# Column copies on VectorE written as one-element maxima, with loads, sums and column counts rearranged, in a one-core graph-network kernel

## The chip, the core and the metric

The kernel runs on one core of one Trainium2 chip. The metric is the device time of the whole program in microseconds. Before the change it is 4877.81 us, the median of three runs (4875.6 to 4879.19). The profile comes from one further execution, taken with the hardware profiler on; that execution took 3555.16 us. So the profiled execution is shorter than the runs without a profile by 1322.6 us, and both numbers are kept apart in what follows.

The engines are called PE (TensorE), DVE (VectorE), ACT (ScalarE), POOL (GpSimd) and SP (SyncE, which here only issues transfers).

## What is computed

One layer of a graph network over 12500 nodes of 64 features and 400000 edges, sorted by their target node `dst`. For each edge the features of both ends and 16 edge features go through two small layers, the messages are summed by target node, and a third layer, a residual and a layer norm finish it:

```python
m_in = concatenate([x[src], x[dst], edge_attr], axis=-1)      # 400000 x 144
h = silu(m_in @ W1 + b1)
messages = silu(h @ W2 + b2)
agg = segment_sum(messages, dst, num_segments=12500)
out = silu(concatenate([x, agg], axis=-1) @ W3 + b3)
return layernorm(x + out)
```

All of it is in float32.

## The kernel before

**Tiles, octets, windows.** Edges are cut into 3125 tiles of 128. Eight tiles make an octet (391 of them), and 24 tiles, three octets, make a window: since the edges are sorted, all targets of a window lie within 112 neighbouring nodes. A loop in `windows` (L555) goes over the octets as a software pipeline: in step o it issues loads for octet o + 2, gathers for o + 3, the first layer of o, the second layer of o - 1 and the sums of o - 2. The order of instructions on PE, ACT, DVE and SP inside that loop is the order in which the code stands; nothing is rescheduled there.

**First layer.** `x[dst] W1b` is formed once a window for its 112 nodes (`window_product` L353, from a slice `xr` of the transposed x that `window_load` L346 brings), and then spread to the edges by a product with a 0/1 matrix `oh`, which `compare_dst` (L377) makes on DVE; the edge features ride in the same matrix's last 16 rows. `x[src] W1a` is precomputed for all nodes in the first octets (`table`, L171) and stored in DRAM as `pa`. For each tile of an octet one indirect transfer, issued by POOL (`gather`, L332, the instruction at L341), fetches 128 rows of `pa`, one for each edge; PE adds them in by a product with the identity (L415). From octet 9 on (`RAW`) the gathers read `pa`, before that x itself.

**Columns and rows.** Not all rows are gathered. The whole transposed x also lies in SBUF (`xs`, 128 partitions, two copies of the 64 features, loaded piece by piece by `resident`, L167). For some pairs of tiles the kernel copies the column of each edge's source node out of `xs`, four bytes of 64 partitions at a time, at an address that is read from a register, into a tile `cx` (`columns`, L244, the copy at L267); PE then multiplies `cx` with W1a (L412). A pair of tiles takes 256 such columns and saves two gathers. ACT makes 28 + 28 columns an octet and DVE 24 + 24 (`ACOLS`, `VCOLS`), in two bursts each: ACT's ahead of its two activations (L419, L434), DVE's behind its two comparisons (L381, L388). Source addresses are loaded into registers 16 at a time on ACT and up to 128 at a time on DVE (L263). The pairs served so are spaced by `RATE`, the sum of all four numbers. SP serves others by single row transfers (`rows`, L280, 16 an octet).

```python
for e, r in zip(range(e0 % P, e0 % P + n), regs):
    copy(t[h, 4 * e:4 * e + 4], xb[h, ds(r - (XBASE[s] + XADDR), 4)])
```

**Second layer and sums.** PE applies W2 (L430), ACT silu (L434), and `add_up` (L439) sums an octet's messages into the window's 112 nodes by a product with another 0/1 matrix `eh`, made by `compare_nodes` (L385) on DVE from the window's node numbers (`wrow`, kept in PSUM) and the edge's target (`dc`, in SBUF). There are four `eh` buffers. When a window's last octet is summed, DVE adds its sums to `agg` in SBUF (`add_window`, L446). `sums` has two halves, used by even and odd windows.

**Nodes.** When all edges of a group of 512 nodes are done, the third layer, the silu, the statistics and later the division and the store of that group are run between octets; `later` (L522) puts each of them at a fixed octet behind `lead`, the octet at which the needed window begins. There are 25 groups.

**Buffers and queues.** A gather needs a free one of five `ga` tiles, so POOL runs three octets ahead. SP issues, in order, the loads of `dr` (the targets, for `oh`), of `oh`'s edge features, of `xr`, the pieces of `xs`, of the targets `dc` and the row transfers. ACT issues the weights at the start and the 25 stores of `pa`.

At the end of the loop (L612 to L635) DVE checks with a few long instructions that the windows did hold all targets; a general path stands behind that check and isn't taken with this data.

Of the kernel before, what the change touches and what calls it, by code (L numbers as in the profile page):

```python
# [14 lines left out]
OP = mybir.AluOpType  # L15
AX = mybir.AxisListType
PSUM = bass.MemoryType.PSUM
DRAM = bass.MemoryType.DRAM
ENG = mybir.EngineType
# [6 lines left out]
SCT = 240  # L26
AHEAD = 3
RAW = 9
TABLES = 5
ACOLS = (28, 28)  # L30
VCOLS = (24, 24)
ROWS = 16
ALOAD = 16
XBASE = (0, 64 << 18)
XADDR = 35840
# [59 lines left out]
def windows(ctx, tc, ident, badi, pa, x, xt, src_c, src_row, dst_c, dst_row, attr_t, base, w1, b1, w2, b2, w3, b3, out, edges):  # L95
    nc = tc.nc
    N, D = x.shape
# [22 lines left out]
    dc = fast.tile([P, TILES], I32, name="dc")  # L120
# [9 lines left out]
    for s in range(2):  # L130
        h = slice(s * D, (s + 1) * D)
# [12 lines left out]
    for s in range(3):  # L144
        part = const.tile([1, D], BF16, name=f"part{s}")
# [19 lines left out]
    xs = fast.tile([P, NP], F32, name="xs")  # L165

    def resident(s, c):  # L167
        w = min(XC, NP - c)
        nc.sync.dma_start(xs[s * D:(s + 1) * D, c:c + w], xt[:, c:c + w])

    def table(c):  # L171
        n = min(4 * P, N - c)
# [38 lines left out]
    for k in range(3):  # L211
        t = fast.tile([P, D], F32, name=f"xw{k}")
# [3 lines left out]
    octs = []  # L216
# [3 lines left out]

    with tc.tile_pool(name="gat", bufs=AHEAD + 2) as gat, tc.tile_pool(name="drp", bufs=2) as drp, \
            tc.tile_pool(name="hot", bufs=3) as hot, \
            tc.tile_pool(name="ehp", bufs=4) as ehp, \
            tc.tile_pool(name="work", bufs=2) as work, tc.tile_pool(name="win", bufs=2) as win, \
            tc.tile_pool(name="ps1", bufs=2, space=PSUM) as ps1, \
            tc.tile_pool(name="ps2", bufs=2, space=PSUM) as ps2, \
            tc.tile_pool(name="psa", bufs=1, space=PSUM) as psa, \
# [5 lines left out]

        RATE = sum(ACOLS) + sum(VCOLS)
        pairs = []
        while True:
            o = RAW + -(-2 * P * (len(pairs) + 1) // RATE) + 1
# [4 lines left out]
        xb = xs.bitcast(U8)  # L242

        def columns(o, eng, part):  # L244
            if o < RAW:
                return
            lo = (o - RAW) * RATE
            if eng == ENG.Activation:
                lo, n, copy = lo + sum(ACOLS[:part]), ACOLS[part], nc.scalar.copy
            else:  # L250
                lo, n, copy = lo + sum(ACOLS) + sum(VCOLS[:part]), VCOLS[part], nc.vector.tensor_copy
            hi = lo + n
            while lo < hi:
                j, e0 = lo // (2 * P), lo % (2 * P)
                if j >= len(pairs):
                    return
                n = min(hi - lo, P - e0 % P, ALOAD if eng == ENG.Activation else P)
                if pairs[j] not in cols:
                    cols[pairs[j]] = cx.tile([P, P], F32, name="cx")
                t = cols[pairs[j]].bitcast(U8)  # L260
                s = e0 // P
                h = slice(s * D, (s + 1) * D)
                _, regs = nc.values_load_multi_w_load_instructions(  # L263
                    indices[j][0:1, e0:e0 + n], engines=(eng,), min_val=XBASE[s] + XADDR,
                    max_val=XBASE[s] + XADDR + 4 * (N - 1), skip_runtime_bounds_check_because="src names a node")
                for e, r in zip(range(e0 % P, e0 % P + n), regs):
                    copy(t[h, 4 * e:4 * e + 4], xb[h, ds(r - (XBASE[s] + XADDR), 4)])  # L267
                lo += n


# [1 line left out]
        while True:  # L272
            o = RAW + -(-2 * P * (len(rpairs) + 1) // ROWS) + 1
# [31 lines left out]
        def raddress(o):  # L305
            yes, j = rbegun(o)
            if yes:
                nc.vector.tensor_scalar(rindex[j], rindex[j], 4.0 * D, None, op0=OP.mult)
# [37 lines left out]
        def window_load(c):  # L346
            regs = nc.values_load(bi[0:1, c:c + 1], engines=(ENG.SP, ENG.DVE), min_val=0, max_val=N - 1,
                                  skip_runtime_bounds_check_because="dst names a node")
            winreg[c] = regs
            xr = win.tile([D, W], F32, name="xr")  # L350
            nc.sync.dma_start(xr, xt[:, ds(regs, W)])
            winrow[c] = xr

        def window_product(c):
            pw = mis.tile([P, D], F32, name="mm")
            nc.tensor.matmul(pw[0:W, :], winrow[c], w1ab[:, 1, :], start=True, stop=True)  # L356
            winrow[c] = pw
# [19 lines left out]
        def compare_dst(o):  # L377
            c, t0, n, first, last = octs[o]
            n2 = n + n % 2
            dr, oh = loaded.pop(o)  # L380
            nc.vector.tensor_tensor(oh[0:W, :n2 * P], dr[:, :n2 * P], wn[0:W, c:c + 1].to_broadcast([W, n2 * P]),  # L381
                                    op=OP.is_equal)
            hots[o] = [oh]
# [62 lines left out]
        def add_window(c):  # L446
            a = agg[:, ds(winreg[c], W)]
            nc.vector.tensor_tensor(a, a, sums[:, c % 2, :], op=OP.add)  # L448
# [4 lines left out]
        RB = 6  # L453
# [63 lines left out]
        due = [-(-(c + n + LAG) // STEP) for c, n in groups]  # L517
        NO = len(octs)
        lead = {c: o for o, (c, t, n, first, last) in enumerate(octs) if first}
        todo = {}  # L520

        def later(o, f, *a):  # L522
            todo.setdefault(min(o, NO), []).append((f, a))
# [1 line left out]
        early = sum(d < NCH for d in due)  # L525
        rest = early - early % RB
        for q in range(early):
            o = lead[due[q]] + 2
            later(o, node_load, q)
            later(o, node_product, q)  # L530
            later(o, node_silu, q)
            later(o + 1, node_stats, q)
        for q0 in range(0, rest, RB):
            o = lead[due[q0 + RB - 1]] + 2
            later(o + 2, root, q0, q0 + RB)
            later(o + 3, inverse, q0, q0 + RB)
            for r in range(RB):
                later(o + 3 + 2 * r, divide, q0 + r)
                later(o + 4 + 2 * r, store, q0 + r)

        for o in range(min(AHEAD, NO)):
            gather(o)
# [9 lines left out]
        with tc.manual_schedule(engines={ENG.PE, ENG.Activation, ENG.DVE, ENG.SP}):  # L552
            compare_dst(0)
            compare_nodes(0)
            for o in range(NO + 1):  # L555
                if o == 0:
                    sources(0, slice(CT, SCT))
                    nc.sync.dma_start(dc[:, CT:SCT], dst_c[:, CT:SCT])
                for k in parts[2 * o - 2:2 * o] if o else []:
                    n = min(XC, NP - k)  # L560
                    nc.scalar.activation(agg[:, k:k + n], zero.to_broadcast([P, n]), AF.Copy)
                if o < 5:
                    for c in parts[:3] if o == 0 else parts[o + 2:o + 3]:
                        resident(0, c)
                if o == 8:
                    nc.sync.dma_start(dc[:, SCT:], dst_c[:, SCT:])
                if o == RAW:
                    nc.vector.memset(mv, 1.0)
                    nc.vector.memset(eps, 1e-5)
                if 5 <= o < 5 + (len(parts) + 1) // 2:  # L570
                    for c in parts[(o - 5) * 2:(o - 4) * 2]:
                        resident(1, c)
                index(o + 3)
                rload(o + 3)
                if o % (SCT // OT) == 6 and (o // (SCT // OT) + 1) * SCT < TILES:
                    sources(o // (SCT // OT) + 1)
                if o + AHEAD < NO:
                    gather(o + AHEAD)
                if o + 2 < NO:
                    load(o + 2)  # L580
                    if octs[o + 2][3]:
                        window_load(octs[o + 2][0])
                if o + 1 < NO:
                    compare_dst(o + 1)
                columns(o, ENG.DVE, 0)
                if o >= 3 and octs[o - 3][4]:
                    add_window(octs[o - 3][0])
                if o < NO:
                    first_layer(o)
                if o + 1 < NO:  # L590
                    if octs[o + 1][3] and o:
                        window_copy(octs[o + 1][0])
                    compare_nodes(o + 1)
                columns(o, ENG.DVE, 1)
                if o >= 1:
                    for c in tables[(o - 1) * per:o * per]:
                        table(c)
                if o >= 2:
                    add_up(o - 2)
                if o >= 1:  # L600
                    second_layer(o - 1)
                if o + 2 < NO and octs[o + 2][3]:
                    window_product(octs[o + 2][0])
                address(o + 2)
                raddress(o + 2)
                rows(o)
                if o < NO:
                    for f, a in todo.get(o, []):
                        f(*a)
# [25 lines left out]
        nc.vector.tensor_copy(badi, bs)  # L635

        add_up(NO - 1)
        for o in range(NO - 2, NO):
            if octs[o][4]:
                add_window(octs[o][0])  # L640
        for f, a in todo.get(NO, []):
# [262 lines left out]
```

## Time and profile before

| | |
|---|---|
| median of three runs | 4877.81 us |
| profiled execution, its own time | 3555.16 us |
| span of its instructions | 3553.3 us |
| granted PE clock, mean | 0.752 |
| POOL: gathers | 2773, of which 2701 from `pa` and 72 from x |
| ACT: column copies | 21112, busy 2079.2 us |
| DVE: column copies | 18056, busy 1458.6 us |
| DMA engines, mean busy share | about a third, 92 GB/s |

A line of the costliest groups names the source line, the engine, the operation, output and inputs, the count, then the busy time in us and the mean duration of one in ns, and behind the second bar the idle time of the engine just before these instructions with what ended most of it. Durations of copies overlap, so busy time is less than count times duration. In a list of waits each line gives who waited for whom, the total in us, how often, and the longest. A line in order of time begins with the start and the length in us; several instructions of a kind are merged, with their count at the end. A line of one source line's instructions gives the count, the shortest, median and longest duration in ns, and the times of the first and the last start.

The busy shares over the 40 slices of the span are even from the second slice on (PE 7 or 8 tenths, DVE 6 or 7, ACT 7 or 8, POOL 7): the loop over octets is nearly the whole program, and one octet stands for all.

### The profile page before, as it was taken

The page shows a single profiled execution, that of the slowest core. Times are in us where ns is not written, and L with a number is a line of the kernel's source. Part 1 is how long each engine was busy: PE and PEld are TensorE (multiplying, and loading weights), DVE is VectorE, ACT ScalarE, POOL GpSimd, SP SyncE. Part 2 cuts the span into 40 slices and gives each one's busy share as a digit, 9 for nine tenths or more (in the row PEclk, how much of TensorE's full clock was granted, in tenths as well). Part 3 has the DMA queues.
Part 4 walks back from the last instruction along what each step waited for, and adds up shares of the span by engine and source line. Part 5 has one row for each costly group of instructions (what it writes and reads, how often), then busy time and mean ns, then how long its engine had stood idle before and what let it go on. Part 6 is the DMA issues. An engine that isn't in the chain of part 4 may idle for free.

```text
span 3553.3 us, 96997 instructions
## 1 busy us (share of the span) xinstructions
PE 2717.1 (76%) x15387; PEld 1796.0 (51%) x15387; DVE 2551.0 (72%) x19955; ACT 2598.8 (73%) x21941; POOL 2659.2 (75%) x2782
## 2 busy tenths in 40 slices
PE   7877877777777778777777777777877777777786
PEld 5554554555545455455454554544544545545454
DVE  3667767777687677776777777777778777677673
ACT  1568777787787777777877777778778777777772
POOL 7677777777777777777777777777777777777774
PEclk7867777777777777777777777777677777777776
DMA  6433333333333333333333333333333333333331
GB/s 158 131 90 95 86 89 92 84 92 90 88 99 91 91 89 85 95 86 89 96 93 94 91 85 93 91 89 89 86 95 94 90 92 86 91 90 87 90 95 47
DMA packets 199259, 327.19 MB, mean 92 GB/s; under 512 B 94959, under 2 KB 103306, under 8 KB 197722
## 3 DMA queue, kind: packets, MB, share of 16 engines
q1 hardware_dynamic: 96142, 226.51, 20.3%
q0 software_dynamic: 88736, 91.04, 13.8%
q10 hardware_dynamic: 13740, 3.32, 0.4%
q14 instruction: 511, 4.19, 0.4%
q8 instruction: 130, 2.13, 0.3%
HBM read 314.20 MB, written 6.40 MB: 90 GB/s over the span
## 4 chain that ended last, share of the span: by engine, by line
POOL 50%; issue 20%; DMA 17%; PE 12%; ACT 1%; DVE 0%; SPq 0%; ACTq 0%; POOLq 0%; DVEq 0%
POOL ga L341 50%; DMA ga<-pa,sc 16%; PE p L430 3%; PE pg L443 2%; PE p L401 2%; PE p L415 1%; PE mm L177 1%; PE p L428 1%; ACT cx L267 1%; PE mm L477 1%; PE mm L476 1%; DMA ga<-in_x,sc 0%; PE p L410 0%; PE p L412 0%; PE mm L406 0%
## 5 line engine op out<-in xcount | busy, mean ns | idle before, releaser
L341 POOL DMA_INDIRECT ga<-pa,sc x2701 | 2589.9, 959 | 838.8 <-issue 746.9
L267 ACT COPY cx<-xs 64x4 uint8 x21112 | 2079.2, 188 | 216.8 <-issue 172.0
L267 DVE COPY cx<-xs 64x4 uint8 x18056 | 1458.6, 204 | 204.4 <-issue 172.7
L415 PE MATMUL p<-ident,ga 128*128 128x128 f32 x2702 | 616.8, 349 | 784.2 <-DMA ga<-pa,sc 781.4
L415 PEld LDWEIGHTS p<-ident,ga 128*128 128x128 f32 x2702 | 461.4, 233 | 1109.6 <-issue 945.6
L430 PE MATMUL p<-w2d,h 128*128 128x128 f32 x3126 | 621.9, 361 | 0.0
L419 ACT ACTIVATE h<-p,b1s 128x512 f32<-128x512 f32 x391 | 268.2, 686 | 480.6 <-PE p L415 437.4
L430 PEld LDWEIGHTS p<-w2d,h 128*128 128x128 f32 x3126 | 530.0, 256 | 127.0 <-issue 127.0
L401 PE MATMUL p<-oh,xw 128*64 128x512 f32 x1564 | 561.8, 806 | 5.5 <-DMA sc<-in_src_c 5.5
L388 DVE TENSOR_TENSOR eh<-wrow,dc 128x896 f32<-128x896 f32 x391 | 424.7, 1086 | 178.9 <-PE pg L443 165.3
L443 PE MATMUL pg<-eh,m 128*64 128x112 f32 x6250 | 528.5, 329 | 14.0 <-ACT m L434 13.9
L381 DVE TENSOR_TENSOR oh<-dr,wrow 112x1024 f32<-112x1024 int32 x391 | 473.1, 1210 | 28.2 <-DMA dr<-in_dst_row 16.8
L443 PEld LDWEIGHTS pg<-eh,m 128*64 128x64 f32 x6250 | 420.3, 178 | 83.5 <-issue 42.4
L434 ACT ACTIVATE m<-p 128x512 f32<-128x512 f32 x391 | 232.6, 595 | 116.2 <-PE p L430 83.0
L428 PE MATMUL p<-b2r,one 3*128 3x512 bf16 x391 | 190.3, 487 | 0.0
L360 DVE COPY xw<-mm 112x64 f32<-112x64 f32 x131 | 29.0, 222 | 208.5 <-PE mm L356 208.5
L448 DVE TENSOR_TENSOR agg<-agg,pg 128x112 f32 x131 | 35.0, 267 | 193.5 <-PE pg L443 184.8
L412 PEld LDWEIGHTS p<-cx,w1d 128*128 128x128 f32 x306 | 56.7, 233 | 188.6 <-issue 188.6
L401 PEld LDWEIGHTS p<-oh,xw 128*64 128x64 f32 x1564 | 94.0, 165 | 60.3 <-issue 23.7
L483 ACT ACTIVATE z<-mm 128x256 f32<-128x256 f32 (+1 forms) x25 | 9.6, 383 | 115.3 <-PE mm L477 115.3
L412 PE MATMUL p<-cx,w1d 128*128 128x128 f32 x306 | 91.3, 388 | 0.0
L341 POOL DMA_INDIRECT ga<-in_x,sc x72 | 68.1, 946 | 22.7 <-issue 20.6
(73 smaller groups left out, 790.2 us busy)
## 6 DMA issues: line engine op xcount, KB each, us to landing
dr<-in_dst_row SPq DMA_DIRECT2D x390, 448.0 KB
rx<-pa SPq DMA_DIRECT2D x5888, 0.2 KB
ga<-pa,sc POOLq DMA_INDIRECT x2701
oh<-in_attr_t SPq DMA_DIRECT2D x390, 64.0 KB
xs<-in_xt SPq DMA_DIRECT2D x12, 512.0 KB
xr<-in_xt SPq DMA_DIRECT2D x131, 28.0 KB
pa<-v ACTq DMA_DIRECT2D x24, 128.0 KB
xa<-in_x SPq DMA_DIRECT2D x24, 128.0 KB
```

Source lines behind the costliest of these rows:

```text
L267: copy(t[h, 4 * e:4 * e + 4], xb[h, ds(r - (XBASE[s] + XADDR), 4)])
L341: nc.gpsimd.indirect_dma_start(out=ga[:, i, :], out_offset=None, in_=x if o < RAW else pa[:, :], in_offset=bass.IndirectOffsetOnAxis(ap=sc ...
L381: nc.vector.tensor_tensor(oh[0:W, :n2 * P], dr[:, :n2 * P], wn[0:W, c:c + 1].to_broadcast([W, n2 * P]), op=OP.is_equal)
L388: nc.vector.tensor_tensor(eh[:, :n], winrow[c][:, None, :].to_broadcast([P, n, W]), dc[:, t0:t0 + n, None].to_broadcast([P, n, W]), op=OP. ...
L401: nc.tensor.matmul(p1[s * D:(s + 1) * D, :k], xw[c % 3], ohv[:, s, :k], start=True, stop=False, skip_group_check=True)
L412: nc.tensor.matmul(p1[:, 0, :], w1d, cols.pop(o), start=False, stop=False, skip_group_check=True)
L415: nc.tensor.matmul(p1[:, i, :], g2.rearrange("p s d -> p (s d)"), ident, start=False, stop=(i == k - 1), skip_group_check=True)
L419: nc.scalar.activation(h[:, :k], p1[:, :k], AF.Silu, bias=b1s)
L428: nc.tensor.matmul(p2[:, :n2, :], one3, b2r[:, :n2, :], start=True, stop=False, skip_group_check=True)
L430: nc.tensor.matmul(p2[:, 2 * i:2 * i + 2, :].rearrange("p s d -> p (s d)"), h[:, i, :], w2d, start=False, stop=(i == k - 1), skip_group_ch ...
L434: nc.scalar.activation(m[:, :n2], p2[:, :n2], AF.Silu)
L443: nc.tensor.matmul(pg[s * D:(s + 1) * D, :], m[:, i, :], eh[:, i, :], start=(first and i < 2), stop=(last and i >= n - 2), skip_group_chec ...
```

## The change

On DVE the column copy becomes a tensor_reduce with maximum over an added innermost axis of length one: the same four bytes of 64 partitions are read and written. ACT keeps its copy. ACT makes 32 + 32 columns an octet and DVE 28 + 24, so `RATE` rises from 104 to 116. The pieces of `xs` and the second part of `dc` are issued from ACT's queue instead of SP's. The slice `xr` of a window is loaded an octet earlier, with a third buffer; its product with W1b stands at the beginning of the next step of the loop instead of near the end of the step before. The add to `agg` and all node work come an octet later, and there is a fifth `eh` buffer. In the changed program POOL has 2737 gathers, ACT 24172 and DVE 19604 columns.

```diff
-ACOLS = (28, 28)
-VCOLS = (24, 24)
+ACOLS = (32, 32)
+VCOLS = (28, 24)
...
     def resident(s, c):
         w = min(XC, NP - c)
-        nc.sync.dma_start(xs[s * D:(s + 1) * D, c:c + w], xt[:, c:c + w])
+        nc.scalar.dma_start(xs[s * D:(s + 1) * D, c:c + w], xt[:, c:c + w])
...
-            tc.tile_pool(name="ehp", bufs=4) as ehp, \
-            tc.tile_pool(name="work", bufs=2) as work, tc.tile_pool(name="win", bufs=2) as win, \
+            tc.tile_pool(name="ehp", bufs=5) as ehp, \
+            tc.tile_pool(name="work", bufs=2) as work, tc.tile_pool(name="win", bufs=3) as win, \
...
                 for e, r in zip(range(e0 % P, e0 % P + n), regs):
-                    copy(t[h, 4 * e:4 * e + 4], xb[h, ds(r - (XBASE[s] + XADDR), 4)])
+                    to, frm = t[h, 4 * e:4 * e + 4], xb[h, ds(r - (XBASE[s] + XADDR), 4)]
+                    if eng == ENG.DVE:
+
+                        nc.vector.tensor_reduce(to, frm[:, :, None], AX.X, OP.max)
+                    else:
+                        nc.scalar.copy(to, frm)
...
         for q in range(early):
-            o = lead[due[q]] + 2
+            o = lead[due[q]] + 3
             later(o, node_load, q)
             later(o, node_product, q)
             later(o, node_silu, q)
-            later(o + 1, node_stats, q)
+            later(o + 2, node_stats, q)
         for q0 in range(0, rest, RB):
-            o = lead[due[q0 + RB - 1]] + 2
-            later(o + 2, root, q0, q0 + RB)
-            later(o + 3, inverse, q0, q0 + RB)
+            o = lead[due[q0 + RB - 1]] + 3
+            later(o + 3, root, q0, q0 + RB)
+            later(o + 4, inverse, q0, q0 + RB)
             for r in range(RB):
-                later(o + 3 + 2 * r, divide, q0 + r)
-                later(o + 4 + 2 * r, store, q0 + r)
+                later(o + 4 + 2 * r, divide, q0 + r)
+                later(o + 5 + 2 * r, store, q0 + r)
...
                 if o == 8:
-                    nc.sync.dma_start(dc[:, SCT:], dst_c[:, SCT:])
+                    nc.scalar.dma_start(dc[:, SCT:], dst_c[:, SCT:])
...
                 if o + 2 < NO:
                     load(o + 2)
-                    if octs[o + 2][3]:
-                        window_load(octs[o + 2][0])
+                if o + 3 < NO and octs[o + 3][3]:
+                    window_load(octs[o + 3][0])
+                if o and o + 1 < NO and octs[o + 1][3]:
+                    window_product(octs[o + 1][0])
                 if o + 1 < NO:
                     compare_dst(o + 1)
                 columns(o, ENG.DVE, 0)
-                if o >= 3 and octs[o - 3][4]:
-                    add_window(octs[o - 3][0])
+                if o >= 4 and octs[o - 4][4]:
+                    add_window(octs[o - 4][0])
...
-                if o + 2 < NO and octs[o + 2][3]:
-                    window_product(octs[o + 2][0])
...
         add_up(NO - 1)
-        for o in range(NO - 2, NO):
+        for o in range(NO - 3, NO):
             if octs[o][4]:
                 add_window(octs[o][0])
```

More of the change, by code (lines that the diff above doesn't have):

```diff
@@ L248, in columns @@
             if eng == ENG.Activation:
-                lo, n, copy = lo + sum(ACOLS[:part]), ACOLS[part], nc.scalar.copy
+                lo, n = lo + sum(ACOLS[:part]), ACOLS[part]
             else:
-                lo, n, copy = lo + sum(ACOLS) + sum(VCOLS[:part]), VCOLS[part], nc.vector.tensor_copy
+                lo, n = lo + sum(ACOLS) + sum(VCOLS[:part]), VCOLS[part]
             hi = lo + n
```

## The prediction, made before the changed kernel was run

> **What bounds the kernel now.** I read the engines' busy time first, then the chain of waits, the costliest groups, the waits of single engines, and last the order of time around the column copies.
>
> ```profile
> span 3553.3 us, 96997 instructions
> ...
> PE 2717.1 (76%) x15387; PEld 1796.0 (51%) x15387; DVE 2551.0 (72%) x19955; ACT 2598.8 (73%) x21941; POOL 2659.2 (75%) x2782
> ...
> POOL 50%; issue 20%; DMA 17%; PE 12%; ACT 1%; DVE 0%; SPq 0%; ACTq 0%; POOLq 0%; DVEq 0%
> ...
> L341 POOL DMA_INDIRECT ga<-pa,sc x2701 | 2589.9, 959 | 838.8 <-issue 746.9
> L267 ACT COPY cx<-xs 64x4 uint8 x21112 | 2079.2, 188 | 216.8 <-issue 172.0
> L267 DVE COPY cx<-xs 64x4 uint8 x18056 | 1458.6, 204 | 204.4 <-issue 172.7
> ```
>
> POOL looks only 75% busy, but its idle time is "issue": after each gather 0.30 us in which it waits for nothing. Gathers follow each other at 0.94 + 0.30 = 1.247 us nearly all the time, and 2773 x 1.247 = 3458 of the 3553 us. So in this execution POOL's gathers set the pace: 391 octets, 7.1 gathers and 9.1 us an octet.
>
> But the profiled execution took 3555.2 us, and the runs without a profile 4877.8: 1322.6 us more, 3.38 us an octet. Such an octet lasts 12.4 us. No engine's own work fills that: PE has 6.95 us an octet at a granted clock of 0.752, 10.4 if it were 0.5 throughout; ACT has 6.6, DVE 6.5, POOL 8.8 with its gaps. Something must hold one engine back for another, and more so without the profiler. The trace shows one such thing. First POOL, then DVE, near the end, in order of time (start, us):
>
> ```profile
> 3478.69 0.95 POOL L341 DMA_INDIRECT ga<-pa,sc  x1 [0.30 <-issue]
> 3479.94 5.15 POOL L341 DMA_INDIRECT ga<-pa,sc  x1 [0.30 <-issue]
> ...
> 3494.13 1.00 POOL L341 DMA_INDIRECT ga<-pa,sc  x1 [0.30 <-issue]
> 3495.43 0.94 POOL L341 DMA_INDIRECT ga<-pa,sc  x1 [0.30 <-issue]
> ```
> ```profile
> 3480.87 3.40 DVE L614 TENSOR_TENSOR xs<-dc,wb 128x3120 f32<-128x3120 int32 x1
> ...
> 3494.22 3.40 DVE L624 TENSOR_REDUCE lim<-xs 128x1 f32<-128x3125 f32 x1
> ```
>
> A gather beside a 3.40 us tensor_tensor with both inputs in SBUF takes 5.15 us instead of 0.94; beside a TENSOR_REDUCE of the same 3.40 us it takes 1.00. So DVE and POOL share something, and a reduce doesn't take it. And the copies:
>
> ```profile
> 1803.13 1.89 DVE L267 COPY cx<-xs 64x4 uint8 x24
> 1803.16 0.94 POOL L341 DMA_INDIRECT ga<-pa,sc  x1 [0.30 <-issue]
> ...
> 1804.40 0.94 POOL L341 DMA_INDIRECT ga<-pa,sc  x1 [0.30 <-issue]
> ```
> ```profile
> L267 DVE COPY cx<-xs x18056: 149/175/477, 127.4 to 3465.4; 64x4 uint8 x199
> ```
>
> Here the gathers aren't delayed, the copies are: 149 ns at best, up to 477, and in the trace it is those that start 0.5 to 0.7 us into a gather that are long. They start every 71 ns, so the sharing exists for copies too; with the profiler on, the copy gives way.
>
> **The change, part by part.** *Copies become maxima (18056 of them).* The Trainium skill, SBUF — State Buffer, Who interferes with whom, says that a VectorE copy between SBUF places can take the port pair that GpSimd shares, exclusively, so that whoever comes second fully blocks, and that a tensor_reduce on trn2 never does. (It also infers that a tensor_tensor leaves descriptor writing alone; the 5.15 us speak against that.) By this trace's rows the edit is worth little: 2773 gathers took 2658 us where 0.944 each makes 2618, so 40 us of delay in all, 4 of it L614's; I take 30. By the rule, if DVE comes first, POOL stands still for whole bursts: two bursts of 24 an octet, 24 x 71 ns = 1.70 us, 752 bursts = 1282 us. The missing time is 1322.6. The two agree within 3%, and I find no other candidate; so for the runs without a profile I take the rule, for the profiled one the rows. Bounds: 30 and 1322 us.
>
> The skill also has a rule against the edit: VectorE: DVE Perf Modes, Rules for kernel authors, calls tensor_reduce the slowest VectorE operation, always one element a cycle. From the rows:
>
> ```profile
> L624 DVE TENSOR_REDUCE lim<-xs x1: 3401/3401/3401, 3494.2 to 3494.2; 128x1 f32<-128x3125 f32 x1
> ```
> ```profile
> L626 DVE TENSOR_REDUCE lim<-xs x1: 280/280/280, 3516.7 to 3516.7; 128x1 f32<-128x131 f32 x1
> ```
>
> (3401 - 280) / (3125 - 131) = 1.04 ns an element, so 280 - 131 x 1.04 = 143 ns are fixed, and four elements take 147 ns: a copy's 149. By the rule the loss is 2 ns x 19604 = 40 us of DVE, off the path. What no row shows is how closely short reduces follow one another. From below: as copies, 71 ns (81 with burst ends: 1458.6 / 18056). From above: 190 ns, from L626's start to the next instruction's in the trace. I take 81, since the fixed part is a copy's.
>
> *More columns.* ACT 56 to 64 an octet, DVE 48 to 52: the build has 24172 and 19604 instructions, 18 more pairs of tiles, and 2737 gathers for 2773. 36 x 1.247 = 45 us off POOL. ACT gets 3060 more at 2079.2 / 21112 = 98.5 ns, 301 us: 2599 + 172 (issue) + 301 = 3072 of some 3480 us, hidden by waits for PE before `h` (437 us now). If that cover were gone it would cost the 301.
>
> *DVE's room.* These waits stand on DVE's queue:
>
> ```profile
> DVE xw L360 <- PE mm L356: 208.5, 103, 4.5
> ...
> DVE agg L448 <- PE pg L443: 184.8, 76, 9.2
> ...
> DVE eh L388 <- PE pg L443: 165.3, 94, 7.5
> ```
>
> The add to `agg` an octet later takes away most of the second, the fifth `eh` buffer most of the third; behind both stood the comparisons and the columns, so DVE gains up to 350 us, but POOL, which sets the pace, nothing: 0 us. The x W1b product is issued on PE just behind the same second layer as before, so the `xw` wait stays; its load on SP goes out an octet earlier, past one `dr` and `oh` pair, and SP waits 348 us for PE at L372 anyway: 0, at worst 131 x 0.3 us on an idle queue. DVE after: 2551 + 1548 x 0.081 + 172 + 208 = 3056 us. The rest, 430 us over 19604, is 22 ns: above 103 ns a reduce, DVE is late next.
>
> *Node work an octet later.* 25 groups, same instructions, their loads on SP included; only the last group could show at the end: 0 to +5 us, taken as 0.
>
> *x and dst over ScalarE's queue.* 14 loads at 477 ns and one at 563 leave SP and go to ACT: 7 us on an ACT that is 18 us busy in the first 90, behind which the first `h` and the stores of `pa` queue. In return SP brings `dr` and `oh` sooner; POOL once waits 15.3 us for an `oh` load near 102 us, but the same gather also needs `pa` stored. Bounds -15 and +7; I take 0.
>
> Sum for the profiled execution: 3555 - 45 - 30 = 3480. Without the profiler: the same, plus up to 41 us of the gap that the bursts don't explain; half of it: about **3490**.
>
> **The rivals.** *The bursts are gone, but short reduces follow more slowly than copies* and DVE sets the pace: 1472 us of other DVE work (3056 - 19604 x 0.081) + 19604 x 0.105 to 0.125 = 3530 to 3920. For it: no short reduce in a row in the trace. Against: the fixed part of 143 ns.
>
> *The gap of 1322 us isn't the copies'* (the edit doesn't do what it is for). For it: no gather in the trace is stopped by a burst. Then 75 us go, or 62 + 41 at the slower pace: about 4800. Against: the 3% agreement, and that no engine fills 12.4 us.
>
> *Slower: reduces don't overlap at all* and start every 190 ns: 1472 + 19604 x 0.19 = 5200. It decides from (4878 - 1472) / 19604 = 174 ns on. For it: the row behind L626; against it: copies of 149 ns do overlap, every 71.
>
> **Numbers.** Likeliest 3490: 0.68. DVE-bound, 3530 to 3920: 0.13. Gap not the copies', about 4800: 0.11. Slower, about 5200: 0.08. The range holds the first two: from 3330 (the likeliest with gathers at 1.20 us without the profiler: 2737 x 0.047 = 129 less, and 30 for the start) to 3920. Faster by over 0.2%, about what a measurement can tell from no change: 0.90; within it 0.02 (from the third case); slower 0.08.
>
> **What would show it.** Right: the run without a profile falls to within 2% of the profiled one; about 2737 gathers at 1.247 us, few over 1 us; no reduce stretched to 477 ns; reduces start every 71 to 85 ns; `eh` and `agg` waits nearly gone. Wrong: the profiled execution at 3480 and the runs still near 4800 (third case); DVE over 90% busy and POOL waiting for PE (second and fourth).

## The result: slower by 4.2%

The changed kernel takes 5087.79 us (median of four runs, 5077.27 to 5095.28), the kernel before, in the same session, 4878.5 (4875.6 to 4888.26): ratio 1.0424, 95% interval 1.04 to 1.0447. The prediction was 3490 us with a range of 3330 to 3920. It was wrong in sign and in size.

The page of the changed kernel, its first lines, the shares of its chain, and the groups that answer to those of before:

```profile
span 5093.2 us, 101788 instructions
...
PE 2857.8 (56%) x15387; PEld 1913.0 (38%) x15387; DVE 2558.9 (50%) x21539; ACT 3073.2 (60%) x25001; POOL 2584.4 (51%) x2746
...
ACT 2%; PE 1%; issue 1%; DVE 0%; another core or an unknown queue 0%; ACTq 0%; DVEq 0%
...
L346 POOL DMA_INDIRECT ga<-pa,sc x2665 | 2515.1, 944 | 2400.2 <-PE p L420 1352.2
L272 ACT COPY cx<-xs 64x4 uint8 x24172 | 2593.3, 188 | 1405.1 <-issue 1361.9
L270 DVE TENSOR_REDUCE cx<-xs 64x4 uint8 x19604 | 1441.6, 156 | 999.8 <-issue 926.2
```

Read the durations first. A gather takes 944 ns (before 959), an ACT column 188 (188), a maximum 156: none of these has become longer. Only PE's busy time has, 2857.8 against 2717.1 us, at a granted clock of 0.674 against 0.752; e14 and e18 below part the clock from the rest. What has grown by far more is idle time: ACT stands 1361.9 us in front of its columns for "issue" (172.0 before), DVE 926.2 (172.7), although nothing that the profile shows holds them; and POOL, which waited almost only for its own issue before, waits 1352.2 us for PE at L420, which must free its `ga` tiles. The chain breaks off after 4% of the span and tells nothing here. Unlike in the page of before, the profiled execution (5095.28 us) agrees with the other runs of its session.

What the idle time looks like, in order of time (start, us):

```profile
1801.23 0.94 POOL L346 DMA_INDIRECT ga<-pa,sc  x1 [0.30 <-issue]
1801.42 0.19 ACT L272 COPY cx<-xs 64x4 uint8 x1 [0.52 <-issue]
1801.42 0.15 DVE L270 TENSOR_REDUCE cx<-xs 64x4 uint8 x1 [0.56 <-issue]
1802.13 0.19 ACT L272 COPY cx<-xs 64x4 uint8 x1 [0.53 <-issue]
1802.14 0.15 DVE L270 TENSOR_REDUCE cx<-xs 64x4 uint8 x1 [0.57 <-issue]
1802.48 0.94 POOL L346 DMA_INDIRECT ga<-pa,sc  x1 [0.30 <-issue]
...
1802.83 0.70 SPq L375 DMA_DIRECT2D dr<-in_dst_row  x1
1802.85 0.19 ACT L272 COPY cx<-xs 64x4 uint8 x1 [0.52 <-issue]
1802.85 0.15 DVE L270 TENSOR_REDUCE cx<-xs 64x4 uint8 x1 [0.56 <-issue]
```

ACT and DVE start one instruction each every 0.71 us, within some 10 ns of each other, SP starts one within 20 ns of them where it has one, and then they stand. POOL goes on at 1.25 us a gather. I call such a stretch a hold. Counting the stretches of over 0.5 us in which none of SP, ACT and DVE starts anything, the trace of before has 241 with 294 us in all, the changed one 2457 with 1894 us; 1779 of these last 0.6 to 0.75 us. Such a count also takes in ordinary waits, so it is compared only between traces of the same kernel or of near ones.

### The profile page after: what moved, and what is told of

Same layout as the page of the kernel before. It is cut to its first block, busy times and chain, and to the rows that moved or that the text cites. A ratio compares the mean times of both kernels' runs of the same rounds, so it can differ in the third digit from the quotient of the medians.

```text
span 5093.2 us, 101788 instructions
## 1 busy us (share of the span) xinstructions
PE 2857.8 (56%) x15387; PEld 1913.0 (38%) x15387; DVE 2558.9 (50%) x21539; ACT 3073.2 (60%) x25001; POOL 2584.4 (51%) x2746
## 5 line engine op out<-in xcount | busy, mean ns | idle before, releaser
L346 POOL DMA_INDIRECT ga<-pa,sc x2665 | 2515.1, 944 | 2400.2 <-PE p L420 1352.2
L272 ACT COPY cx<-xs 64x4 uint8 x24172 | 2593.3, 188 | 1405.1 <-issue 1361.9
L270 DVE TENSOR_REDUCE cx<-xs 64x4 uint8 x19604 | 1441.6, 156 | 999.8 <-issue 926.2
L448 PE MATMUL pg<-eh,m 128*64 128x112 f32 x6250 | 609.2, 365 | 2130.9 <-ACT m L439 803.9
L448 PEld LDWEIGHTS pg<-eh,m 128*64 128x64 f32 x6250 | 487.1, 201 | 2211.8 <-ACT m L439 843.3
L435 PE MATMUL p<-w2d,h 128*128 128x128 f32 x3126 | 714.7, 400 | 0.0
L435 PEld LDWEIGHTS p<-w2d,h 128*128 128x128 f32 x3126 | 615.1, 293 | 150.7 <-issue 150.7
L406 PE MATMUL p<-oh,xw 128*64 128x512 f32 x1564 | 613.6, 876 | 4.3 <-issue 4.3
L420 PEld LDWEIGHTS p<-ident,ga 128*128 128x128 f32 x2666 | 406.5, 230 | 257.0 <-issue 232.5
L420 PE MATMUL p<-ident,ga 128*128 128x128 f32 x2666 | 464.0, 323 | 0.1
```

The lines of the kernel that those rows point to most:

```text
L270: nc.vector.tensor_reduce(to, frm[:, :, None], AX.X, OP.max)
L272: nc.scalar.copy(to, frm)
L346: nc.gpsimd.indirect_dma_start(out=ga[:, i, :], out_offset=None, in_=x if o < RAW else pa[:, :], in_offset=bass.IndirectOffsetOnAxis(ap=sc ...
L406: nc.tensor.matmul(p1[s * D:(s + 1) * D, :k], xw[c % 3], ohv[:, s, :k], start=True, stop=False, skip_group_check=True)
L420: nc.tensor.matmul(p1[:, i, :], g2.rearrange("p s d -> p (s d)"), ident, start=False, stop=(i == k - 1), skip_group_check=True)
L435: nc.tensor.matmul(p2[:, 2 * i:2 * i + 2, :].rearrange("p s d -> p (s d)"), h[:, i, :], w2d, start=False, stop=(i == k - 1), skip_group_ch ...
```

## The theories

A: the holds belong to where a kernel runs, not to the change; the page of before came from one kind of place and its timed runs from another. A1: the row transfers on SP cause the holds. A2: loads of addresses or of instructions do. B, the prediction's: VectorE's copies lock POOL out. C: the changed kernel makes the holds itself. D: in a slow place all engines together issue a fixed 19.5 to 20 instructions a us.

The eighteen runs below fell on seven chips. The kernel before took 3553 to 3568 us on four (numbers 3, 4, 6, 13) and 4877, 4968 and 4990 us on three (5, 0, 10), and on a chip all kernels were of the same kind. I call these quick and slow chips. Each chip was used in one stretch of time only, though, so something about the chip and something about that time (other work beside it, say) can't be told apart here. Every ratio is to the kernel before on the same chip, in turns.

## The experiments on a quick chip: the change in parts

**e1, the kernel before again.**

> The kernel before, unchanged, with a profile of its own. In the changed kernel's trace SP, ACT and DVE again and again start nothing for some 0.7 us and then go on within 20 ns of each other; gaps of over 500 ns in their merged starts add up to 1894 us, against 294 us in the profile of before that the prediction was made from. Theory A (common stalls of these three engines make the difference between 3555 and 4878 us, in both kernels): this profile, if its execution takes about 4880 us, has some 1600 us of such gaps, and gathers of still 0.94 us. Theory B (copies on VectorE lock POOL out): gathers beside copies are stretched, mean well over 1.2 us, and the gaps stay near 300 us.

3567.91 against 3568.24 us, ratio 1.0003 (0.9989 to 1.0017); 230 common holds with 292 us. It is the page of before, without a gap between the profile and the other runs.

**e2, the maxima alone**, with 56 and 48 columns an octet:

```diff
-                    copy(t[h, 4 * e:4 * e + 4], xb[h, ds(r - (XBASE[s] + XADDR), 4)])
+                    to, frm = t[h, 4 * e:4 * e + 4], xb[h, ds(r - (XBASE[s] + XADDR), 4)]
+                    if eng == ENG.DVE:
+                        nc.vector.tensor_reduce(to, frm[:, :, None], AX.X, OP.max)
+                    else:
+                        nc.scalar.copy(to, frm)
```

> The kernel before with VectorE's copies as maxima and nothing else. Theory B, as predicted: about 3500 us. Theory A: about 4880 us, since a maximum takes as long as a copy (it starts every 64 to 71 ns in the trace of the changed kernel) and the stalls do not ask what the instruction computes.

3517.24 us, ratio 0.9852 (0.9834 to 0.9869): 51 us less. The time between the starts of gathers beyond 1.247 us sums to 71.7 us in e1 and 23.2 in e2, so 48.5 of the 51 us come from there. Some gathers are indeed shut out by copies: 91 of e1's take over 1.2 us, against one in e2. The longest in both stands beside the 3.40 us tensor_tensor that the prediction shows; the longest beside copies, in e1, in order of time:

```profile
247.72 2.10 POOL L341 DMA_INDIRECT ga<-pa,sc  x1 [0.30 <-issue]
247.92 1.78 DVE L267 COPY cx<-xs 64x4 uint8 x24
```

So copies do lock POOL out, as theory B has it, but for most of a burst only at two gathers of 2773 (2.10 and 2.07 us), and all of it together is worth 51 us.

**e3, everything but the maxima**: the changed kernel with a tensor_copy on DVE.

> The changed kernel with VectorE's copies left as copies. Theory A: about 5090 us, as the changed kernel, because the rest (more columns, loads on ACT, one octet later) makes the difference. Theory B: slower than the changed kernel by some hundred us.

3521.0 us, ratio 0.9869 (0.9852 to 0.9885): 47 us less, where 36 gathers were to give 45.

**e4, the kernel before without SP's row transfers**: `rpairs` stays empty, and their rows are gathered, 46 gathers more.

```diff
-        while True:
-            o = RAW + -(-2 * P * (len(rpairs) + 1) // ROWS) + 1
-            if o >= len(octs) - 1:
-                break
-            rpairs.append(o)
```

> The kernel before without SP's single row transfers (16 an octet); POOL gathers these rows, 46 gathers more (57 us). Theory A1 (SP's row transfers are what the three engines wait for together): the common gaps nearly go, the time falls to about 3650 us. Theory A2 (the stalls come from elsewhere, for example from fetching instructions or from the address loads on ACT and DVE): 4800 to 4950 us.

3625.84 us, ratio 1.0159 (1.0141 to 1.0178): 57.6 us more, as 46 x 1.247 = 57.4 us of gathers. On a quick chip this says nothing yet on A1. (The count of holds is 522 with 707 us here, presumably since SP no longer starts its rows inside ordinary waits.)

**e12, the changed kernel again**, on a quick chip.

> The changed kernel, again. On a chip with the kernel before at about 3570 us: 3470 us (3568 less 51 for the maxima and 47 for the rest, if the two add up), ratio 0.973; if the cost of the added columns holds there too, at 41 ns each, 3470 + 190 = 3660, ratio 1.026. On a slow chip: ratio 1.04 as three times before.

3474.2 us (3473.06 to 3481.19) against 3553.15, ratio 0.9785 (0.9768 to 0.9801): here the change is 2.15% *faster*. Its page, the same lines as above:

```profile
span 3471.9 us, 101788 instructions
...
PE 2711.7 (78%) x15387; PEld 1790.9 (52%) x15387; DVE 2474.6 (71%) x21539; ACT 2914.0 (84%) x25001; POOL 2588.9 (75%) x2746
...
L346 POOL DMA_INDIRECT ga<-pa,sc x2665 | 2519.6, 945 | 828.0 <-issue 728.9
L272 ACT COPY cx<-xs 64x4 uint8 x24172 | 2420.1, 188 | 149.0 <-issue 109.6
L270 DVE TENSOR_REDUCE cx<-xs 64x4 uint8 x19604 | 1357.9, 159 | 278.7 <-issue 197.7
```

The same 101788 instructions, gathers, columns and maxima with the same durations (945, 188 and 159 ns against 944, 188 and 156), in 1621 us less. ACT's issue is 109.6 us instead of 1361.9, and POOL hardly waits for PE any more. There are 218 holds with 230 us, so the two pages differ by 1664 us of holds. They also differ in the granted PE clock, 0.757 against 0.674, and in PE's busy time by 146 us. C falls: on this chip the same kernel has next to no holds.

**e16, maxima and new column counts, without the moved loads, products and sums.**

```diff
-ACOLS = (28, 28)
-VCOLS = (24, 24)
+ACOLS = (32, 32)
+VCOLS = (28, 24)
```

and the lines of e2.

> The kernel before with the maxima and the new column counts, without the moves of loads, products and sums. On a quick chip: 3474 us (ratio 0.9785, as the whole change) if the moves are worth nothing there, as the prediction put them; up to 3517 (0.985, maxima alone) if the 47 us beside the maxima belong to the moves. On a slow chip 1.039 as before.

3470.07 us, ratio 0.9756 (0.9737 to 0.9775), on another quick chip than e12. The whole change has 0.9785 (0.9768 to 0.9801), so no gain of the moves shows; the two intervals just meet.

**e11, the kernel before, for a page of its own on a slow chip.** It ran on a quick one.

> The kernel before, again, for its page on this chip. On a chip that runs the kernel before in about 3570 us: common stalls of SP, ACT and DVE of some 300 us in all, as in the first such run. On one that takes 4880 to 4990 us: every theory but the lock expects some 1700 us of common stalls (those of the changed kernel, 1894 us, less its loss of about 200), gathers still 0.94 us long, and the waits of ACT and DVE called issue several times the 172 us of the page of before. The lock (copies keep POOL out) expects gathers far longer than 0.94 us instead.

3558.33 against 3553.15 us, ratio 1.0009 (0.9998 to 1.002), 234 holds with 287 us. So the kernel before has no page from a slow chip; e8, e9 and e10 below stand nearest to it.

## The experiments on slow chips: what the holds answer to

**e5 and e7, the changed kernel again.**

> The changed kernel, unchanged. Where before takes 3568 us (as in the last four runs), theory A (5088 and 4878 us were both made of common stalls of SP, ACT and DVE that belong to where the runs were made, not to the kernels) expects 3470 to 3490 us: 2737 gathers at 1.247 us and no stretched ones, with gaps of over 500 ns in the merged starts back at some 250 us. Theory C (the changed kernel makes the stalls itself, and before only catches them sometimes) expects about 5090 us and 1900 us of such gaps again. Where before takes 4878 us, both expect about 5090.

> The changed kernel, unchanged, once more: chips differ, and it has been run so far only where before takes 4880 to 4970 us. Where before takes 3568 us, theory A and theory D (below) expect 3470 to 3490 us with some 250 us of common gaps; theory C (the changed kernel makes the stalls itself) about 5090. Where before is slow, a ratio of 1.042 again.

5183.45 against 4967.59, ratio 1.0424 (1.0389 to 1.0459) on chip 0; 5187.48 against 4989.61, ratio 1.0386 (1.0335 to 1.0438) on chip 10. The result repeats on both slow chips on which the changed kernel ran again, and not on the quick one (e12).

**e6, maxima and new column counts without the moves** (the kernel of e16).

> The kernel before with the maxima and with 64 and 52 columns an octet, but loads on SP, the sums and node work at their old places. Where before takes 3568 us: 3517 (maxima alone) less 36 gathers of 1.247 us, so about 3472, if ACT and DVE have room; up to 3530 if the wait of DVE for the sums and for the fourth buffer of eh comes to stand on the path. Where before takes 4878 us: near 5090 if the added 4608 instructions on ACT and DVE are what makes the changed kernel the slower one there.

5155.35 us, ratio 1.0386 (1.0362 to 1.041), beside 1.0424 for the whole change on that chip. So most of the loss is made by e2's edit and the 4608 more columns; what is left for the moves, 0.4%, lies within the intervals.

**e10, the maxima alone** (the kernel of e2).

> The kernel before with VectorE's copies as maxima alone, the same number of instructions. Theory D: within 0.5% of before where before is slow, and 1.5% faster where it is fast, as measured. Theory B (copies lock POOL out on the slow chips): 1300 us faster there.

5050.46 us, ratio 1.0108 (1.0051 to 1.0165): 61 us more. This is what B stands or falls by. By B the copies' lock makes up the 1322 us, and maxima would bring the kernel to some 3500 us on this chip. They bring no gain but a loss of 0.5 to 1.7%, of which no run shows the cause. The kernel itself is held here and not on e2's chip: 2761 holds with 2135 us against 263 with 316, and a span of 5056.8 us against 3516.4. VectorE's copies themselves, on the same slow chip, in the page of e8 below:

```profile
L341 POOL DMA_INDIRECT ga<-pa,sc x2701 | 2580.6, 955 | 2564.3 <-PE p L415 1801.3
L267 ACT COPY cx<-xs 64x4 uint8 x21112 | 2248.8, 188 | 1313.6 <-issue 1265.3
L267 DVE COPY cx<-xs 64x4 uint8 x18056 | 1570.4, 193 | 930.4 <-issue 905.8
```

Beside 18056 copies a gather takes 955 ns, 959 in the page of before, and the longest of e8's takes 1387 ns (the view of that line's durations). A gather shut out for a whole burst of 24 x 71 ns would take over 2600. So B doesn't make the 1322 us.

**e8, 24 tiny products and weight loads more an octet** on PE, 18768 instructions in all, overwritten by the real product behind them:

```diff
+            for _ in range(24):
+                nc.tensor.matmul(p2[:, 0, 0:16], one3, b2r[:, 0, 0:16], start=True, stop=True, skip_group_check=True)
```

> The kernel before with 24 tiny matmuls (3 rows, 16 columns) and their weight loads ahead of each bias product, 18768 instructions more on PE, which is idle over a third of the time where before is slow. Theory D (on the slow chips the time is the number of executed instructions of all engines at a fixed rate: 96997 in 4878 and 101788 in 5088 us are 19.9 and 20.0 per us, and 19.5 and 19.6 on the second slow chip): 18768 / 19.6 = 957 us more there, so about 5900; where before takes 3568, under 3650. Theory A (only SP, ACT and DVE are held, by something of their own): under 100 us more on either chip.

5319.63 us, ratio 1.065 (1.0598 to 1.0703): 330 us more. A fixed total rate wanted 957, so D as stated falls, and so does "under 100". The slow pages confirm it: instructions over span are 10.5 a us in e18, 18.0 in e9, 19.2 in e10 and 21.7 here, no fixed rate. It doesn't give a price for an instruction: in the order of time 24 such products take 0.80 us of PE, 391 x 0.80 = 313 us in all, and I didn't run it on a quick chip. It does show that PE is held too:

```profile
1807.92 0.18 PEld L401 LDWEIGHTS p<-oh,xw 128*64 128x64 f32 x1 [1.23 <-issue]
1808.62 0.28 ACT L267 COPY cx<-xs 64x4 uint8 x2 [1.15 <-issue]
1808.62 0.23 DVE L267 COPY cx<-xs 64x4 uint8 x2 [1.19 <-issue]
1808.64 0.59 PE L401 MATMUL p<-oh,xw 128*64 128x512 f32 x1 [0.44 <-issue]
1808.68 0.13 PEld L401 LDWEIGHTS p<-oh,xw 128*64 128x64 f32 x1 [0.57 <-issue]
1809.37 0.19 ACT L267 COPY cx<-xs 64x4 uint8 x1 [0.47 <-issue]
1809.37 0.17 DVE L267 COPY cx<-xs 64x4 uint8 x1 [0.52 <-issue]
```

**e9, no row transfers** (the kernel of e4).

> The kernel before without SP's row transfers, 12306 instructions fewer (84691). Theory D: 84691 / 19.6 = 4320 us where before takes 4970, 3626 where it takes 3568. Theory A1 (SP's row transfers cause the stalls): 3650 to 3750 on both. Theory A2 (address loads on ACT and DVE cause them): within 2% of before where before is slow.

4708.5 us, ratio 0.9429 (0.9381 to 0.9477): 281 us less, although its 46 gathers more cost 57 us on a quick chip. The holds remain (2453 with 2048 us, against e4's 522 with 707), so A1 falls. A2 had no run of its own, but the trace of the result speaks against it: a load of addresses by ACT or DVE is under way in 31% of its 2457 holds, and in 64% of stretches of the same lengths laid at random; a transfer that loads instructions in 13%, and in 16% of those. Where the rows cost the 281 us is less clear. One wait goes with them (total in us, times, longest). In e10, on the same chip and with the rows:

```profile
DVE oh L385 <- DMA dr<-in_dst_row: 827.3, 215, 8.8
```

In e11, with the rows on a quick chip:

```profile
DVE oh L381 <- DMA dr<-in_dst_row: 12.3, 18, 1.7
```

The loads of `dr` stand on SP's queue behind 16 rows, whose transfers start every 0.60 us in the mean in e10 and every 0.41 in e11. Without the rows this wait is gone from e9's list. But on chip 0 the changed kernel (e5) has 221.1 us of the same wait where e6 has 505.7, and it isn't the quicker of the two; so that this wait makes the 281 us is not shown.

## The reverse of the change: fewer instructions

**e13, no columns on DVE**: `VCOLS = (0, 0)`, 19349 instructions fewer in all, with 142 gathers more.

> The kernel before without DVE's columns: 18056 DVE instructions fewer and 141 gathers more. If the time on a slow chip is set by the number of instructions at some 40 ns for a column, it gets quicker there by 18056 x 0.041 = 740 us, to about 4200 (ratio 0.85), and on a quick chip slower by 141 x 1.247 = 176 us, less up to 50 for gathers that DVE's copies no longer stretch, to 3700 to 3745 (1.04 to 1.05). If a slow chip's stalls are a fixed share of the time, it gets slower on both: 1.03 to 1.05.

A quick chip: 3695.46 us, ratio 1.0396 (1.0379 to 1.0413); 142 x 1.247 = 177 us of gathers, less the 50 that copies cost gathers, makes 127, and 142 were measured.

**e14, e15, e17 and e18, 16 columns an octet and no rows**: `ACOLS = (8, 8)`, `VCOLS = (0, 0)` and e4's edit, 49237 instructions instead of 96997. Three of the four ran on quick chips.

> The kernel before with 16 columns an octet, all on ACT, and no row transfers: some 33000 columns and 12000 SP instructions fewer, about 3080 gathers. POOL needs 3080 x 1.247 = 3840 us, and some 80 beside: 3920 us wherever POOL is the bound. If instructions of SP, ACT and DVE are what a slow chip stalls on, the stalls shrink until POOL is the bound there too: 3920 to 4100 us on either chip, ratio 0.79 to 0.84 on a slow one and 1.10 on a quick one. If the stalls go with time and not with instructions: 1.05 to 1.10 on both.

> As e14 (16 columns an octet, no row transfers), in the hope of a slow chip. There, if the stalls shrink with the instructions of SP, ACT and DVE: 3890 (as on the quick chip) to 4100 us, ratio 0.79 to 0.84. If they go with time: ratio 1.05 to 1.10. On a quick chip again: 1.096.

> As e14 (16 columns an octet, no row transfers). On a slow chip, if the stalls shrink with the instructions of SP, ACT and DVE: 3890 (as on a quick chip) to 4100 us, ratio 0.79 to 0.84. If they go with time: ratio 1.05 to 1.10. On a quick chip again: 1.096.

> As e14 (16 columns an octet, no row transfers). On a slow chip, if the stalls shrink with the instructions of SP, ACT and DVE: 3890 (as on a quick chip) to 4100 us, ratio 0.79 to 0.84. If they go with time: ratio 1.05 to 1.10. On a quick chip again: 1.096.

On chips 3, 13 and 4: 3894.52, 3897.96 and 3899.24 us, ratios 1.096 (1.0942 to 1.0979), 1.0954 (1.0932 to 1.0976) and 1.0963 (1.0941 to 1.0985). On chip 5, slow: 4675.43 against 4877.01 us, ratio 0.9586 (0.9561 to 0.961). That is neither expectation: the sign turns round, as fewer instructions were to do, but 780 us remain over the quick chips instead of 0 to 200. Both pages, first a quick chip's (e14), then the slow one's (e18):

```profile
span 3896.6 us, 49237 instructions
...
PEclk7876776776777776777777776767767677677766
...
L336 POOL DMA_INDIRECT ga<-pa,sc x3007 | 2842.0, 945 | 928.2 <-issue 823.5
```
```profile
span 4677.3 us, 49237 instructions
...
PEclk6677777777777777677777777767777777776766
...
L336 POOL DMA_INDIRECT ga<-pa,sc x3007 | 2848.6, 947 | 1656.9 <-issue 784.6
```

POOL's gathers take the same time, and the granted PE clock is alike (0.721 and 0.719 in the mean), so the clock doesn't make the 780 us. With most of the columns and all rows gone it is PE that is held, one weight load in 0.71 us:

```profile
2001.11 0.13 PEld L396 LDWEIGHTS p<-oh,xw 128*64 128x64 f32 x1 [0.71 <-PE p L425]
2001.83 0.13 PEld L396 LDWEIGHTS p<-oh,xw 128*64 128x64 f32 x1 [0.58 <-issue]
2002.54 0.13 PEld L396 LDWEIGHTS p<-oh,xw 128*64 128x64 f32 x1 [0.58 <-issue]
2003.26 0.13 PEld L396 LDWEIGHTS p<-oh,xw 128*64 128x64 f32 x1 [0.59 <-issue]
```

Two such steps of 0.69 to 0.735 us in a row occur 211 times among PE's starts in e18, never in e14, never in the changed kernel's own slow page, and 865 times in e8. So A needs mending: the holds aren't those of SP, ACT and DVE alone, they fall on PE too, and where SP, ACT and DVE issue little, mostly on PE: 577 times an instruction of PE's sequencer (mostly weight loads) starts 0.65 to 0.75 us behind the one before it in e18, and 61 times in e14; for ACT it is 182 and 193. Lined up by how densely a kernel issues on a quick chip (instructions over its time there; the kernel before taken at 3560 us):

| kernel | instructions a us, quick chip | time on a quick chip, us | on a slow chip, us (chip) | slow / quick | before, same slow chip / 3560 |
|---|---|---|---|---|---|
| few columns, no rows | 12.6 | 3898 | 4675 (5) | 1.20 | 1.37 |
| no rows | 23.4 | 3626 | 4709 (10) | 1.30 | 1.40 |
| maxima alone | 27.6 | 3517 | 5050 (10) | 1.44 | 1.40 |
| maxima and columns | 29.3 | 3470 | 5155 (0) | 1.49 | 1.40 |
| the change | 29.3 | 3474 | 5187 (10) | 1.49 | 1.40 |

The kernel before issues 27.2 a us and stands at 1.37 to 1.40. The denser a kernel issues where it can, the more a slow chip takes from it. This is an order of six kernels on three chips, not a law; and a kernel that leaves its engines more slack behind POOL on a quick chip has more room for holds before its time grows, which would give the same order.

## Why the prediction was wrong, step by step

**The 1322.6 us between the profile and the runs: the step that failed.** The prediction said that something must hold one engine back, "and more so without the profiler", took whole bursts of VectorE's copies for it (752 x 24 x 71 ns = 1282 us), and leaned on an agreement within 3% with no other candidate. The agreement was chance. With the same instructions, a quick chip takes 3553 to 3568 us and a slow one 4877 to 4990, and in every run the profiled execution agrees with the others; 3555.16 is a quick chip's time and 4877.81 a slow one's. That the two numbers on record came from two chips is inferred from this, since the record names the chip of neither. The working didn't ask that question at all. What fills the time in its place are the holds: on a slow chip the maxima alone gain nothing, and that kernel, the nearest to before with a slow page, is 1540 us longer there, with 1819 us more of holds (e10 against e2). The rule of the Trainium skill (SBUF — State Buffer, Who interferes with whom) gives the shared ports to whoever issues first for the whole instruction; the prediction stretched that to a burst of 24 instructions, and to all 752 bursts. In the traces most copies give way instead, and a gather is shut out for most of a burst twice in e1's 2773. The row, some 40 us of delay in all, was about right on both kinds of chip (959 ns a gather in the page of before, 955 in e8).

**The sum for the profiled execution was right.** 3480 was foretold against the page of before, and a quick chip gives 3474.2. Its terms: the columns -45 us, measured (0.9852 - 0.9756) x 3560 = 34 (e2 against e16); the stretched gathers -30, measured 51 (e2); the moves 0, measured (0.9785 - 0.9756) x 3560 = +10, uncertain by about as much. So copies and gathers do meet, at the small price of the row. That term was too small because the page of before happens to have less of this delay than e1: beyond 944 ns a gather, and without the one at L614, 38.5 us there, of which I took 30, against 55.5 in e1 and 3.3 in e2, on one chip.

**Reduces.** Foretold at 71 to 85 ns apart, they are 63 to 64 apart inside a burst, 1357.9 / 19604 = 69 ns with burst ends where 81 was taken. The changed kernel on the quick chip (e12), one line's durations:

```profile
L270 DVE TENSOR_REDUCE cx<-xs x19604: 133/148/238, 130.1 to 3392.6; 64x4 uint8 x199
```

The longest is 238 ns, a copy's was 477: no wait for POOL shows, as the skill's rule for tensor_reduce has it. The rivals of DVE as the bound (from 105 ns) and of no overlap (from 174) are far off. DVE's sum of 3056 us holds by luck, 2474.6 + 197.7 + 376.4 = 3049: the reduces are cheaper, and the wait of `xw` is dearer.

**DVE's waits**, e12 again:

```profile
DVE xw L365 <- PE mm L361: 376.4, 82, 13.7
...
DVE agg L453 <- PE pg L448: 35.9, 23, 8.0
```

`agg` fell from 184.8 to 35.9 us and `eh` from 165.3 to nothing, as foretold. `xw` was to stay at 208.5 and rose to 376.4. The order of the code suggests why (the copy of the x W1b sums now stands ahead of the comparison in its step, where PE is not yet done); no run moved it alone. POOL noticed neither, also as foretold.

**The cover of ACT's columns, 301 us.** This cost was put at nothing, hidden by 437 us of waits for PE before `h`, with the full 301 if the cover were gone. On the quick chip it is hidden. On a slow one it is gone. e10 and e7, on the same chip, differ by these columns, by 1548 columns on DVE and by the moves. ACT's busy time is 2740.8 and 3081.9 us and its issue wait in front of columns 1351.5 and 1408.6, so ACT's queue carries 398 us more, and the span is 5198.6 - 5056.8 = 142 us longer. The other 61 us of the loss on this chip came with the maxima (e10). Behind ACT's columns stand `h` and `m`, and PE's sums wait for them. PE's sums in the kernel before on a quick chip (e11), with the maxima on a slow chip (e10), and in the changed kernel on the same slow chip (e7):

```profile
PE pg L443 <- ACT m L434: 15.4, 15, 1.8
```
```profile
PE pg L447 <- ACT m L438: 727.1, 145, 13.3
```
```profile
PE pg L448 <- ACT m L439: 922.0, 146, 14.6
```

Most of this wait comes with the slow chip, and 195 us of it with the change, while the sums' wait for ACT's columns themselves falls from 363.4 to 292.6. From there POOL waits for PE to free `ga`, and the 36 gathers saved are worth nothing, for POOL no longer sets the pace. That the 142 us run through this queue is read from the waits and not shown: no run moved the columns behind the activations or added ACT's columns alone.

**The third case, "the gap isn't the copies'", was the right mechanism** and was given 0.11. Its 4800 us were wrong too, because it carried the quick chip's 75 us of gain over to runs that POOL doesn't bound. The point from which "slower" was to decide lay in the reduces; it lay in what bounds the slow runs.

**What stays open.** What makes the holds: a limit on issuing instructions, on writing records of them, or something else of those three chips or of the time at which they were used. Profiled and other runs agree on a slow chip (e18: 4679.04 us, and 4667.48 to 4687.23), but nothing here separates these, and holds can be counted only in a profiled execution. Also open are the 61 us that the maxima cost on a slow chip, and the price of one instruction more: the runs give no single one.

## To carry to other kernels

When a profiled execution and the timed runs differ by a third, first run the same kernel again, on several chips and at several times, before a mechanism is sought: a sum that fills the gap to 3% proves nothing. Read the bound from a page of the kind of run that the time comes from: an edit that relieves the bound on a quick chip (gathers saved by more copies on ACT) loaded ACT's queue, behind which PE waits on a slow one. No kernel tried was best on both: 0.9756 and 1.0386 for the maxima with the new column counts, 1.0159 and 0.9429 for leaving out the row transfers.

## What the runs showed of the hardware that was not expected

- Chips of two kinds, each seen in one stretch of time: the kernel before takes 3553 to 3568 us on four and 4877 to 4990 us on three. In the changed kernel the durations of gathers, columns and maxima are the same on both, and the difference of 1621 us is about that of the holds, 1664 us, most of them of some 0.7 us. SP, ACT, DVE and PE are held. POOL keeps 1.25 us a gather as long as its tiles are free; at that pace a hold of 0.7 us between two instructions need not show.
- Fewer instructions don't free a kernel of it: with half of them gone (e18) PE was held instead, and the time was still 20% longer than on a quick chip.
- On VectorE a maximum of four one-byte elements can follow another after 63 to 64 ns, where a copy follows after 71.
